# First attention: the early queries' values on four quarters of the PE array, with a second PSUM bank

## The chip, the cores and the metric

The kernel runs on one core of one Trainium2 chip. The metric is the device time of one execution in microseconds (us), shown as the median of several runs. The core has five engines with a program of their own each: PE (TensorE, matmuls and transposes; its weight loads are listed apart as PEld), DVE (VectorE), ACT (ScalarE), POOL (GpSimd) and SP (SyncE, here only a DMA queue). Matmuls write to PSUM, which has eight banks of 128 partitions x 512 fp32.

## The reference

A block of two layers on x of 32 sequences x 128 tokens x 128 features. Each layer adds an attention and then a feed-forward part to x, each conditioned on a vector per sequence. The change touches only the attention of the first layer:

```python
qkv = inputs @ W_qkv                       # 128 -> 3 x 16 heads x 64
q, k, v = jnp.split(qkv, 3, axis=-1)       # each reshaped to (b, l, H=16, D=64)
score = jnp.einsum('bihd,bjhd->bijh', q, k) / D ** 0.5
masked_score = score * mask + 1e+30 * (mask - 1.0)      # causal
wmat = jax.nn.softmax(masked_score, axis=2)
out = jnp.einsum('bijh,bjhd->bihd', wmat, v).reshape(b, l, H * D)
return out @ W_out
```

`inputs` is x modulated by the condition. The second layer's attention, its mixture of experts and its slot memory fill the second half of the run and are not touched.

## The kernel before

**Units.** The first attention works in 64 units: 16 values of h (a group g = h // 2 of four sequences, and one half of the 16 heads) times the four sequences b of the group. A unit has one sequence and eight heads. Since the mask is causal, the 64 early queries see only the 64 early keys, the 64 late queries see all 128 keys; the two are computed apart. A unit's eight heads are counted by slot (0 or 1), side (0 or 1) and par (0 or 1): head = 2 * (2 * slot + side) + par.

**Stages of a unit** (function `unit`), each delayed against the one before by a `Staggered` pipe with lags of 0, 3, 4 and 5 units, so that one step of the pipe issues `scores` of unit n, `turned` of unit n - 3, `values` of unit n - 4, and every fourth step `projected`:

- `scores`: 16 matmuls with 64 rows and 64 columns of the array into two banks, one for each par (the row half). The four (row half, column half) combinations follow one another in the order that `k % 2, (k // 2 + k) % 2` gives. Two matmuls add the mask. DVE takes the row maxima (`s_max`), and for the early queries subtracts the maximum into `s_sb` columns 4:6; ACT takes exp, four activations for the late queries and one for the early ones; POOL and DVE form the sums and scale.
- `turned`: six PE transposes of `s_sb` into two banks, four (late) read by one ACT copy, two (early) read by one DVE copy, into `pT`.
- `values`: one bank. Eight matmuls for the late queries (128 rows, 64 columns), then eight for the early ones (64 rows, 64 columns). An early matmul of par 0 uses row half 0 and column half 0, one of par 1 uses row half 1 and column half 1. One DVE copy of 128x512 takes the bank to `oT`.
- `projected`: 4 matmuls with `w_out` over four units' `oT`, added to x by DVE.

A matmul in fp32 stands in the trace as two instructions (a transpose as one), so the early values of a unit are 16 of them.

**V and its shifted copy.** `vv` (L460) keeps V of a sequence as `v` [keys, 8 heads, 64], and an SP DMA copies the early keys of the last four of its heads to partitions 64 to 127 of `vo`, so that row half 1 can work on early keys too. In this kernel the columns of W_qkv are permuted on the host, so that the last four heads in `v` are those of par 1.

**Banks.** Each `ps()` takes the next turn in a ring of eight, whose letters are three tile tags with 2, 3 and 3 banks; a turn waits until a bank of its tag has been read out:

```python
RING = "AABBBCCC"
def ps():
    if short:
        return bank("C")
    turn["all"] += 1
    return bank(RING[(turn["all"] - 1) % 8])
```

`short` is set after the last unit's scores, when the second layer's work begins to use A and B: the last four steps' `turned`, `values` and `projected` then have the three C banks only.

**What else lies in the stage.** Each step of the pipe is followed by three pieces of the next half's projections (`qk`: a 128x512 matmul and an ACT copy, or `v`), each of one turn. A step without anything else takes two turns for `scores`, two for `turned`, one for `values` and three for the pieces: eight. Into some steps the recurrence of the first feed-forward part is put (`recurrence`, seven times in this stage: three turns, sigmoids on ACT, and long DVE reciprocals and scans) or a cycle of its coupling network (`twisted`, seven cycles in this stage: a chain PE, ACT, PE, ACT with Gelu and Tanh, then DVE and POOL). They bring ACT table loads too. Engines' orders are those that the tile framework's scheduler makes out of the program's order and the waits; nearly all bank turns on PE start in the program's order (7 of 615 start ahead of an earlier one).

Of the kernel before, what the change touches and what calls it, by code (L numbers as in the profile page):

```python
# [16 lines left out]
ALU = mybir.AluOpType  # L17
AX = mybir.AxisListType

P = 128  # L20
B = 32
S = 128
D = 128
# [82 lines left out]
def _packs(i):  # L106

    g = lambda n: np.asarray(i[n])
    f = lambda n: g("L1_ffn_" + n)
    cond = g("cond_1024")  # L110
    c = lambda n: g("L1_cond_" + n)
# [39 lines left out]
        ("f_ln_g", _col(f("ln_g"))),  # L151
        ("f_ln_b", _col(f("ln_b"))),
    ]

    qkv = g("L0_attn_W_qkv")
    qkv_v = qkv[:, 2048:].reshape(D, 2, 4, 2, 64).transpose(0, 1, 3, 2, 4).reshape(D, 1024)
    attn0 = [
        ("w_qkv", np.concatenate([qkv[:, :2048], qkv_v], axis=1)),
    ]
    attn0o = [  # L160
        ("w_out", g("L0_attn_W_out").reshape(8, P, D).transpose(1, 0, 2).reshape(P, 8 * D)),
# [83 lines left out]
def program(ctx, tc, out, xT, packs, where):  # L245
# [19 lines left out]
    V, T, G, A = Pinned(nc.vector, pinned), Pinned(nc.tensor, pinned), Pinned(nc.gpsimd, pinned_g), nc.scalar  # L265
# [17 lines left out]
    def w(name):  # L283
        pack, rows, c0, n = where[name]
        return loaded[pack][:rows, c0 : c0 + n]
# [8 lines left out]
    def bank(tag):  # L294
        return psum.tile([P, 512], F32, tag="ps" + tag, name="ps", bufs=RING.count(tag))
# [6 lines that stand above are left out]
# [5 lines left out]
    def mm(out_, lhsT, rhs, start=True, stop=True):  # L307
        T.matmul(out_, lhsT=lhsT, rhs=rhs, start=start, stop=stop)

    def inner(ap, n):  # L310

        return ap.unsqueeze(2).to_broadcast([ap.shape[0], ap.shape[1], n])

    def outer(ap, n):

        return ap.unsqueeze(1).to_broadcast([ap.shape[0], n, ap.shape[1]])

    def tt(eng, out_, a, b, op):
        eng.tensor_tensor(out_, a, b, op)
# [10 lines left out]
    def col(g):  # L330
        return X[:, bass.ts(g, CH)]

    def b3(ap):

        return ap.rearrange("p (b s) -> p b s", s=S)

    def halves(ap):

        return ap.rearrange("p (u t) -> p u t", u=2)
# [34 lines left out]
    def act(*args, **kwargs):  # L374

        return tc.keep_in_program_order(A.activation(*args, **kwargs))  # L376
# [19 lines left out]
    w_qkv, w_out = w("w_qkv"), w("w_out")  # L396
    hTs, qks, vs, oTs = {}, {}, {}, {}
# [75 lines left out]
    def unit(h, b):  # L473

        g = h // 2
        cs = bass.ts(b, S)
        q2 = slice(b * S, b * S + 64), slice(b * S + 64, b * S + S)  # L480
        at = {}
        if b == 0:
            oTs[h] = apool.tile([P, 4, CH], F32, tag="oT", name="oT")

        def scores():

            two = [ps()[:, 0 : 3 * S].rearrange("p (c k) -> p c k", k=192) for par in range(2)]
            for late in (1, 0):
                for slot in range(2):
                    for k in range(4):  # L490
                        par, side = k % 2, (k // 2 + k) % 2
                        r = slice(64 * par, 64 * par + 64)
                        i = 2 * slot + side
                        o = two[par][64 * side : 64 * side + 64, slot, slice(0, S) if late else slice(S, 192)]
                        mm(o, qks[h][2 * i][r, q2[late]], qks[h][2 * i + 1][r, cs if late else q2[0]], start=bool(late) and slot == 0, stop=False)

            for par in range(2):
                mm(two[par][:, :, 64:192], twice16[:, 0, :], outer(causal16.rearrange("p u k -> p (u k)"), 2), start=False)

            s = apool.tile([P, 6, S], F32, tag="s_sb", name="s_sb", bufs=5)  # L500
            m6 = apool.tile([P, 2, 2, 3], F32, tag="s_max6", name="s_max6", bufs=5)
            nm = apool.tile([P, 2, 2], F32, tag="s_max", name="s_max", bufs=5)
            for par in range(2):
                V.tensor_reduce(m6[:, par], two[par].rearrange("p c (n k) -> p c n k", k=64), AX.X, ALU.max, negate=True)
                tt(V, nm[:, par], m6[:, par, :, 0], m6[:, par, :, 1], ALU.min)
                tt(V, s[:, 4:6, bass.ts(par, 64)], two[par][:, :, S:192], inner(m6[:, par, :, 2], 64), ALU.add)
                for slot in range(2):
                    act(s[:, 2 * par + slot], two[par][:, slot, 0:S], AF.Exp, bias=nm[:, par, slot : slot + 1])
            act(s[:, 4:6], s[:, 4:6], AF.Exp)
            sm = apool.tile([P, 8], F32, tag="s_sum", name="s_sum", bufs=5)  # L510
            late, early = s[:, 0:4], s[:, 4:6].rearrange("p c (n k) -> p (c n) k", k=64)
            if h == 2 * NCH - 1 and b >= CB - 2:

                V.tensor_reduce(sm[:, 0:4], late, AX.X, ALU.add)
                V.tensor_reduce(sm[:, 4:8], early, AX.X, ALU.add)
                V.reciprocal(sm, sm)
                tt(V, late, late, inner(sm[:, 0:4], S), ALU.mult)
                tt(G, early, early, inner(sm[:, 4:8], 64), ALU.mult)
            else:
                half = apool.tile([P, 4, 64], F32, tag="s_half", name="s_half")  # L520
                tt(G, half, late[:, :, 0:64], late[:, :, 64:128], ALU.add)
                part = apool.tile([P, 8, 32], F32, tag="s_part", name="s_part")
                tt(G, part[:, 0:4], half[:, :, 0:32], half[:, :, 32:64], ALU.add)
                tt(G, part[:, 4:8], early[:, :, 0:32], early[:, :, 32:64], ALU.add)
                V.tensor_reduce(sm, part, AX.X, ALU.add)
                V.reciprocal(sm, sm)
                tt(G, late, late, inner(sm[:, 0:4], S), ALU.mult)
                tt(G, early, early, inner(sm[:, 4:8], 64), ALU.mult)
            at["s"] = s

        def turned():
            pT = apool.tile([P, 6, S], F32, tag="pT", name="pT", bufs=3)
            p = ps()
            for i in range(4):
                T.transpose(p[:, bass.ts(i, S)], at["s"][:, i, :], ident)
            act(pT[:, 0:4], b3(p), AF.Copy)
            p = ps()
            for i in range(2):
                T.transpose(p[:, bass.ts(i, S)], at["s"][:, 4 + i, :], ident)
            V.tensor_copy(pT[:, 4:6], b3(p)[:, 0:2])  # L540
            at["pT"] = pT

        def values():
            p = ps()
            (v, vo), pT = vs[h][b], at["pT"]
            for late in (1, 0):
                for i in range(4):
                    slot, side = i // 2, i % 2
                    for par in range(2):
                        o = p[64 * par : 64 * par + 64, i * S + 64 * late : i * S + 64 * late + 64]  # L550
                        r = slice(0, P) if late else slice(64 * par, 64 * par + 64)
                        vh = v[r, 4 * par + i, :] if late or not par else vo[r, i, :]
                        mm(o, vh, pT[r, 2 * par + slot if late else 4 + slot, bass.ts(side, 64)])
            V.tensor_copy(oTs[h][:, :, cs], b3(p))

        def projected():
            u = h % 2
            p = ps()
            for m in range(4):
                mm(p, w_out[:, bass.ts(4 * u + m, D)], oTs[h][:, m, :], start=(m == 0), stop=(m == 3))  # L560
            tt(V, col(g), col(g), p, ALU.add)

        return [scores, turned, values] + ([projected] if b == CB - 1 else [])


# [278 lines left out]
    for h in range(NH):  # L844
# [3 lines left out]
        for b in range(CB):  # L848
# [15 lines left out]
            k = h - 6  # L864
# [581 lines left out]
    for r in range(NP):  # L1446
        a, c = 2 * r, 2 * r + 1
# [97 lines left out]
    for i in range(END + 2 * TURN):  # L1545
        r, k = i // TURN, i % TURN
# [62 lines left out]
```

## Time and profile before

| | us |
|---|---|
| median of 3 runs (1238.57 to 1244.77) | 1240.27 |
| profiled execution, its own time | 1240.42 |
| its span, first to last instruction | 1238.6 |
| first attention in it (first scores to last values) | 28 to 602 |
| PE busy | 1091.0 (88%) |
| DVE busy | 754.8 (61%) |
| ACT busy | 695.9 (56%) |
| POOL busy | 447.2 (36%) |

Busy PE is not PE at its peak: matmuls overlap, and their ends are modelled. A wait is read from the timeline, where a row is "start, length, engine, line, operation, out<-in, shape, count" and in brackets how long the engine had been idle and what released it. All helpers' instructions carry the helper's line (L259 for PE, DVE and POOL; L376 for most of ACT), so that they are told apart by the tiles' names: `ps` is any PSUM bank, `s_sb<-ps,s_max` on ACT the exp of late scores, `s_sb<-s_sb` that of early ones, `pT<-ps` the two copies of `turned`, `oT<-ps` that of `values`.

### The profile page before, as it was taken

What the parts mean: (1) busy time and instruction counts of PE and PEld (TensorE: products, weight loads), DVE (VectorE), ACT (ScalarE), POOL (GpSimd) and SP (SyncE); (2) the same over time, 40 slices, a digit from 0 to 9 for tenths busy, and PEclk for the clock granted to TensorE, in tenths of its full rate; (3) what the DMA queues carried; (4) which work ended last, traced back from release to release, by engine and by line L of the source; (5) the groups of instructions that cost most, each with busy time, mean ns of one, the idle gap of its engine ahead of it and who ended that gap; (6) DMA issues with size and microseconds to landing.
All of it is one profiled execution on the core that took longest, in us unless ns stands there. A gap on an engine that the chain in (4) does not pass through costs nothing. (4 is left out here: it accounts for less than half of the span.)

```text
span 1238.6 us, 28745 instructions
## 1 busy us (share of the span) xinstructions
PE 1091.0 (88%) x11429; PEld 696.8 (56%) x11429; DVE 754.8 (61%) x2253; ACT 695.9 (56%) x1668; POOL 447.2 (36%) x556
## 2 busy tenths in 40 slices
PE   6999999979999799888878668998999899998774
PEld 2556554535554355545545345776676676676543
DVE  2556766474884837837355388465756674657554
ACT  2655455555645555526355466666865587568631
POOL 1644545454554545524354531133213321222000
PEclk9999999989999899979989898999999999999867
DMA  7000000000000000000342300233023402320000
GB/s 278 11 10 10 12 8 10 10 4 10 8 10 10 4 7 10 11 3 8 110 121 66 100 26 3 78 112 129 11 78 103 154 12 69 104 67 11 2 17 17
DMA packets 23604, 56.46 MB, mean 46 GB/s; under 512 B 2608, under 2 KB 12976, under 8 KB 23344
## 3 DMA queue, kind: packets, MB, share of 16 engines
q0 software_dynamic: 9504, 38.97, 10.2%
q1 hardware_dynamic: 13248, 14.11, 3.8%
q8 instruction: 90, 1.47, 0.5%
q10 hardware_dynamic: 720, 1.57, 0.4%
q14 instruction: 42, 0.34, 0.1%
HBM read 46.25 MB, written 2.10 MB: 39 GB/s over the span
## 5 line engine op out<-in xcount | busy, mean ns | idle before, releaser
L376 ACT ACTIVATE s_sb<-ps,s_max 128x128 f32<-128x128 f32 x256 | 74.3, 368 | 123.0 <-DVE s_sb L259 116.8
L259 PE MATMUL ps<-hT,w_attn 128*128 128x512 f32 x256 | 128.7, 630 | 8.3 <-ACT s_sb L376 4.7
L259 POOL TENSOR_TENSOR s_sb<-s_sb,s_sum 128x512 f32<-128x512 f32 (+1 forms) x126 | 106.9, 869 | 67.9 <-DVE s_sum L259 54.7
L376 ACT ACT_TABLE_LOAD x63 | 80.8, 1283 | 79.9 <-DVE s_sb L259 53.5
L259 POOL DMA_INDIRECT ew<-in_expert,rows x64 | 63.5, 992 | 130.5 <-DVE ye L259 79.4
L376 ACT ACTIVATE qk<-ps 128x512 f32<-128x512 f32 x128 | 71.9, 610 | 48.6 <-PE ps L259 48.1
L259 POOL TENSOR_TENSOR s_half<-s_sb 128x256 f32<-128x256 f32 x62 | 46.8, 755 | 126.8 <-ACT s_sb L376 112.7
L259 PEld LDWEIGHTS ps<-qk 64*64 64x64 f32 x2048 | 54.6, 136 | 62.7 <-ACT s_sb L376 23.3
L376 ACT ACTIVATE he<-ps,ew 128x128 f32<-128x128 f32 x256 | 71.9, 386 | 31.8 <-issue 18.4
L259 PE MATMUL ps<-pT,v 128*64 128x64 f32 (+1 forms) x1536 | 85.1, 231 | 4.8 <-DVE X L259 3.1
L259 DVE TENSOR_REDUCE s_max<-ps 128x6 f32<-128x384 f32 x128 | 64.4, 540 | 39.0 <-PE ps L259 39.0
L259 PEld LDWEIGHTS ps<-pT,v 128*64 128x64 f32 (+1 forms) x1536 | 71.8, 140 | 23.4 <-issue 4.8
L259 PEld LDWEIGHTS ps<-hT,w_attn 128*128 128x128 f32 x256 | 47.4, 196 | 66.5 <-issue 42.8
L376 ACT ACTIVATE s<-ps,s1max 128x128 f32<-128x128 f32 x256 | 73.3, 391 | 18.9 <-DVE s1max L259 18.8
L259 PE MATMUL ps<-he,ew 128*128 128x128 f32 x512 | 77.1, 291 | 6.0 <-ACT he L376 5.1
L259 PEld LDWEIGHTS ps<-he,ew 128*128 128x128 f32 x512 | 67.9, 197 | 25.2 <-ACT he L376 13.7
L259 PE MATMUL ps<-qk 64*64 64x64 f32 (+1 forms) x2048 | 65.3, 255 | 16.1 <-ACT s_sb L376 13.8
L259 DVE TENSOR_REDUCE s_sum<-s_part 128x8 f32<-128x256 f32 x62 | 25.8, 417 | 84.7 <-POOL s_part L259 84.7
L259 PE MATMUL ps<-X,ew 128*128 128x128 f32 x512 | 76.8, 282 | 0.2 <-DMA ew<-in_expert,rows 0.2
L259 DVE TENSOR_REDUCE s1m<-ps 128x6 f32<-128x384 f32 x128 | 65.0, 548 | 16.2 <-PE ps L259 16.2
L259 PEld LDWEIGHTS ps<-X,ew 128*128 128x128 f32 x512 | 67.0, 193 | 10.4 <-issue 9.0
L259 PE MATMUL ps<-w_base,s 128*128 128x128 f32 x384 | 62.0, 288 | 7.9 <-ACT s L376 4.8
(302 smaller groups left out, 2544.3 us busy)
## 6 DMA issues: line engine op xcount, KB each, us to landing
vo<-v SPq DMA_DIRECT2D x64, 64.0 KB, 1.9
v1o<-v SPq DMA_DIRECT2D x8, 256.0 KB, 3.6
out_x<-ot SPq DMA_DIRECT2D x8, 256.0 KB, 2.3
X<-in_xT ACTq DMA_DIRECT2D x4, 256.0 KB, 9.1
X<-in_xT SPq DMA_DIRECT2D x4, 256.0 KB, 9.1
w_lowr<-in_lowr SPq DMA_DIRECT2D x1, 1024.0 KB
ew<-in_expert,rows POOLq DMA_INDIRECT x64, 5.1
w_ffn<-in_ffn SPq DMA_DIRECT2D x1, 928.0 KB, 8.4
```

The costliest lines, as they stand in the source:

```text
L259: ins = f(*args, **kwargs)
L376: return tc.keep_in_program_order(A.activation(*args, **kwargs))
```

## The change

Early matmuls of `values` use row half = slot and column half = par, all four quarters, in the same order of combinations as `scores`. Those of slot 1 write to a second bank `p2`; those of slot 0 stay in `p` with the late ones. So `values` takes two turns of the ring, and three DVE copies (128x256, and twice 128x128) take the place of one 128x512. The early part of `s_sb` is laid out by par instead of by slot (a DVE output of the same size), and the host no longer permutes the columns of W_qkv: the last four heads of `v`, which the DMA to `vo` copies, are now those of slot 1. The number of matmuls, transposes and DMAs and their sizes stay.

```diff
-    qkv = g("L0_attn_W_qkv")
-    qkv_v = qkv[:, 2048:].reshape(D, 2, 4, 2, 64).transpose(0, 1, 3, 2, 4).reshape(D, 1024)
     attn0 = [
-        ("w_qkv", np.concatenate([qkv[:, :2048], qkv_v], axis=1)),
+        ("w_qkv", g("L0_attn_W_qkv")),
     ]
...
-                tt(V, s[:, 4:6, bass.ts(par, 64)], two[par][:, :, S:192], inner(m6[:, par, :, 2], 64), ALU.add)
+                tt(V, halves(s[:, 4 + par]), two[par][:, :, S:192], inner(m6[:, par, :, 2], 64), ALU.add)
...
         def values():
-            p = ps()
+
+            p, p2 = ps(), ps()
             (v, vo), pT = vs[h][b], at["pT"]
-            for late in (1, 0):
-                for i in range(4):
-                    slot, side = i // 2, i % 2
-                    for par in range(2):
-                        o = p[64 * par : 64 * par + 64, i * S + 64 * late : i * S + 64 * late + 64]
-                        r = slice(0, P) if late else slice(64 * par, 64 * par + 64)
-                        vh = v[r, 4 * par + i, :] if late or not par else vo[r, i, :]
-                        mm(o, vh, pT[r, 2 * par + slot if late else 4 + slot, bass.ts(side, 64)])
-            V.tensor_copy(oTs[h][:, :, cs], b3(p))
+            for i in range(4):
+                for par in range(2):
+                    c = slice(64 * par, 64 * par + 64)
+                    mm(p[c, i * S + 64 : (i + 1) * S], v[:, 2 * i + par, :], pT[:, 2 * par + i // 2, bass.ts(i % 2, 64)])
+            for side in range(2):
+                for k in range(4):
+                    slot, par = k % 2, (k // 2 + k) % 2
+                    i, r, c = 2 * slot + side, slice(64 * slot, 64 * slot + 64), slice(64 * par, 64 * par + 64)
+                    o = p2[c, bass.ts(side, 64)] if slot else p[c, i * S : i * S + 64]
+                    vh = vo[r, 2 * side + par, :] if slot else v[r, 2 * i + par, :]
+                    mm(o, vh, pT[r, 4 + par, bass.ts(side, 64)])
+            o4 = oTs[h][:, :, cs]
+            V.tensor_copy(o4[:, 0:2], b3(p)[:, 0:2])
+            V.tensor_copy(o4[:, 2:4, 64:S], b3(p)[:, 2:4, 64:S])
+            V.tensor_copy(o4[:, 2:4, 0:64], halves(p2[:, 0:S]))
```

## The prediction

> **What bounds the kernel now.** I first read the busy times by stretch, because only the stage of the first attention (28 to 602 us of the span) is touched; the chain that ended last names its pieces only from 804.80 us on, so it says nothing about this stage. Columns are the stretch, its length, then each engine's busy time and count, and the granted clock:
>
> ```profile
> 100.00:150.00 50.00, 47.91 (x526) 28.42 (x526) 37.28 (x86) 26.03 (x63) 26.17 (x36) 1.00 0.03 8
> 150.00:200.00 50.00, 47.97 (x497) 28.00 (x496) 34.71 (x80) 26.54 (x63) 25.43 (x34) 1.00 0.05 12
> 250.00:300.00 50.00, 41.95 (x382) 23.06 (x382) 33.63 (x70) 24.41 (x52) 25.76 (x31) 0.86 0.03 7
> ```
>
> PE is busy 48 of 50 us in most stretches and 42 in some; DVE, the next, 33 to 37. So PE bounds the stage, except where something makes it wait. What does is in the waits of PEld from 50 to 620 us (total, times, longest); the timeline shows two such places, in a recurrence and in a cycle of the coupling network:
>
> ```profile
> PEld ps L259 <- ACT s_sb L376: 34.8, 38, 4.9
> ```
>
> ```profile
> 128.05 1.18 ACT L376 ACTIVATE s_sb<-ps,s_max 128x128 f32<-128x128 f32 x4 [3.08 <-DVE s_sb L259]
> ...
> 128.73 1.05 PE L259 MATMUL ps<-qk 64*64 64x128 f32 x32 [0.62 <-ACT s_sb L376]
> ...
> 129.11 0.42 ACT L376 ACTIVATE s_sb<-s_sb 128x256 f32<-128x256 f32 x1
> ...
> 129.42 0.60 ACT L376 ACTIVATE pT<-ps 128x512 f32<-128x512 f32 x1
> ```
>
> ```profile
> 277.16 1.56 PE L259 MATMUL ps<-qk 64*64 64x128 f32 x32 [4.09 <-ACT s_sb L376]
> ```
>
> The scores read no exp: they wait because the bank they want still holds scores whose exp ACT has not read. The ring explains it. Counting the program's turns, 29 of the 63 steps from one scores to the next have exactly eight, so there scores take the banks of the scores just before.
>
> **What the change does, part by part.** *Early matmuls.* This is the row rhythm of a unit's values before:
>
> ```profile
> 107.41 0.90 PE L259 MATMUL ps<-qk 64*64 64x128 f32 x32
> ...
> 108.24 0.39 PE L259 MATMUL ps<-causal,twice 128*128 128x256 bf16 x2
> ...
> 109.84 0.27 PE L259 MATMUL ps<-pT,vo 64*64 64x64 f32 x1
> ...
> 109.94 0.22 PE L259 MATMUL ps<-pT,vo 64*64 64x64 f32 x1
> ...
> 110.00 0.22 PE L259 MATMUL ps<-pT,vo 64*64 64x64 f32 x1
> ...
> 110.06 0.22 PE L259 MATMUL ps<-pT,vo 64*64 64x64 f32 x1
> ...
> 110.44 0.70 PE L259 MATMUL ps<-X,w_mix 128*128 128x512 f32 x1
> ```
>
> The two diagonal quarters start as a pair every 58 ns, eight pairs. The scores block already uses four quarters in the changed order: read record by record, its 16 early instructions of the same shape start in fours, the fours also 58 ns apart. Eight pairs become four fours: 4 x 58 = 0.23 us less per unit, 64 x 0.23 = **14.9 us** of PE at most. The gap on entering and leaving the 64-row form stays.
>
> *Copies.* Groups from 50 to 620 us (busy, mean ns):
>
> ```profile
> L259 DVE COPY oT<-ps 128x512 f32<-128x512 f32 x64 | 43.7, 682 | 6.7 <-remote 2.8 <-PE ps L259 2.0
> L259 DVE COPY pT<-ps 128x256 f32<-128x256 f32 x63 | 25.8, 410 | 0.0
> L259 DVE TENSOR_TENSOR s_sb<-ps,s_max 128x128 f32<-128x128 f32 x120 | 33.3, 281 | 0.0
> ```
>
> A line through the two copies gives 274 ns for 128x128, and the third row, another operation of that size, 281. So three copies are 410 + 274 + 274 = 958 ns for 682. A DVE instruction starts some 0.08 us before the end of the one ahead (the 0.41 us pT copy at 121.44 us, oT at 121.77), so from end to end it is 958 - 160 = 0.80 us, 0.12 more; ends of the range 0.12 and 0.28. Times 64: 7.7 us of DVE, hidden in most steps, since DVE has 13 to 17 us free in 50. Behind these copies stand the sums and the next maxima, for which ACT and then PE wait. The cover is gone in the seven recurrences, where reciprocals and scans keep DVE busy without a pause over about three units: 7 x 3 x 0.12 = **2.5 us**.
>
> Here a rule of the Trainium skill speaks against the change. "TensorEngine Tiling (Array Packing)", sections PSUM Bottleneck and Gotcha 1, says that tiling speeds TensorE but not the emptying of PSUM, that one access should span several tiles of a bank, and that different row tiles write to different banks. Were emptying the limit everywhere, the sum would be no gain and all 7.7 us lost: 1248.1. The rows do not show that on average, DVE being at 33 to 37 of 50, so I take 2.5. The rule's other half, the bank, is what I take over.
>
> *The second bank.* A plain step now takes nine turns of a ring of eight, and everything slides by one: s0 wants the former s1's bank, s1 that of the last transposes (free after ACT's pT copy), and the last projection piece wants the bank of the s0 of its own step. Steps of more turns slide likewise. On PE, in order, all later work queues behind such a wait: mask, transposes, values, pieces, then ACT's copies. Where ACT is on time this costs nothing: bank hand-overs have a median slack near 3 us before. Where ACT is late:
>
> - Recurrence: at 128.73 us scores start when s0's exps are done; the pT copy ends at 130.02. Wanting that bank, scores start 1.29 later, less the 0.15 that the block already loses inside (1.05 for 0.90): 1.1. In the next step a piece was stopped for 1.14 us at 138.47; one turn more puts one piece more (0.86) behind the same wait. They don't add, as ACT and DVE, which release, did not move: 1.0 per stretch.
> - Coupling cycle: at 277.16 scores wait for s0's exps and crawl (1.56) to 278.65; the pT copy that follows on ACT ends at 278.42. Starting there and taking 0.83, they end at 279.25: 0.6.
>
> Seven of each lie in the stage: 7 x 1.0 + 7 x 0.6 = **11.2 us**. The bounds are nothing (each tag has two or three banks, and whichever is free is taken) and some 24 us (about 24 turns, counted against the trace's release times, would be late by 0.8 to 2 us, if all added at 1.0).
>
> In these 14 stretches PE's saving of about two units each goes into the wait: 28 x 0.23 = 6.5, which leaves 14.9 - 6.5 = **8.4 us** of gain.
>
> *The end.* In the last four steps three C banks serve two transposes and one bank of values; with four, p2 needs the transposes' bank of its own step, hence an ACT copy, 0.6 us: 4 x 0.6 = **2.4 us**, between 0 and 6.
>
> *The rest:* the s_sb layout (281 ns, same size), the host's columns and the DMA to vo (64 KB, same) cost nothing: same instructions, no new wait.
>
> **Sum:** -8.4 + 11.2 + 2.5 + 2.4 = +7.7 us on the profiled execution's 1240.4: **1248**. It stands 0.15 us above the median of the runs, so the forecast for the median is the same.
>
> **Rivals.** *PE's gain comes through.* The order isn't rigid (at 181.98 us transposes went ahead of blocked scores), banks within a tag are interchangeable, and PE is the bound for 48 of 50 us. Then the waits don't lengthen: -14.9 + 2.5 to -8.4 + 2.5, or 1228 to 1234.5. Against it: 29 steps hand scores to scores now, and just these slide. *They cancel:* half of the bank and end cost, 6.8 - 8.4 + 2.5 = +1, 1241. *All late turns add:* every late turn delays PE by itself, +24 + 2.5 + 2.4 - 8.4 = +20, 1261; against it, the releases come from ACT and don't move with PE. *The quarters don't run together* (slot 0 and 1 in different banks, but each shared with other work): no gain, 1248 + 8.4 = 1256; against it, the scores' fours, which also write two banks.
>
> **Chances.** Forecast 0.35, gain comes through 0.25, cancel 0.22, all add 0.13, quarters fail 0.05. About 0.5% (6.2 us) is what a measurement can tell from no change. Faster: 0.25; same: 0.22; slower: 0.35 + 0.13 + 0.05 = 0.53. As signs are mixed: the forecast's own range is 1244 to 1254; the range for 8 in 10, 1231 to 1262, cuts off the better half of the gain and the far end of the adding case.
>
> **What would show it.** Early value records in fours 58 ns apart confirm the saving, pairs refute it. oT copies become 192, about 61 us busy for 43.7. PE's waits for ACT s_sb and pT (34.8 and 6.9 us in PEld's list) should grow by about 10 us, with pieces of qk and v waiting for s_sb. If they stay while the stage ends 8 or more us before 602, the bank step is wrong and the first rival right. If the stage is longer without such waits, the scheduler's order or DVE is the cause.

## The result and the profile after

Before, the median was 1239.83 us (14 runs, 1236.51 to 1244.88), after it 1244.28 us (14 runs, 1240.46 to 1247.66): a ratio of **1.0034, interval 1.0019 to 1.005**. A second series, with 22 runs of the change, gave 1.0031 (1.0019 to 1.0042). So the change costs some 4 to 5 us: a small loss, but one whose interval leaves out 1. The first profiled execution of the change took 1242.46 us (span 1240.7).

The page after, busy time by engine and the granted clock over the span:

```profile
PE 1085.4 (87%) x11429; PEld 686.7 (55%) x11429; DVE 756.7 (61%) x2381; ACT 694.4 (56%) x1668; POOL 446.9 (36%) x556
...
PEclk8999999989999889999889889999999999999867
```

The stretches that the prediction read (length, then busy time and count of PE, PEld, DVE, ACT, POOL, then the clock):

```profile
100.00:150.00 50.00, 47.48 (x528) 27.47 (x528) 36.13 (x98) 26.50 (x64) 25.89 (x36) 1.00 0.03 8
150.00:200.00 50.00, 47.74 (x496) 27.22 (x494) 34.44 (x93) 27.16 (x64) 25.37 (x36) 0.97 0.05 12
250.00:300.00 50.00, 41.51 (x346) 21.32 (x345) 32.64 (x80) 25.91 (x54) 26.82 (x33) 0.90 0.03 6
```

PE is a little less busy, DVE hardly changed, and the second stretch, at full clock before, has lost some. PEld's waits from 50 to 620 us (total, times, longest):

```profile
PEld ps L256 <- ACT s_sb L373: 38.8, 65, 3.2
PEld ps L256 <- DVE pT L256: 25.1, 10, 4.8
```

The wait for exp grew by 4 us and became shorter and more frequent; the wait for DVE's copy into pT, 4.5 us before, is new in this size. The values of a unit, and the copies behind them:

```profile
109.59 0.27 PE L256 MATMUL ps<-pT,vo 64*64 64x64 f32 x1
...
109.60 0.27 PE L256 MATMUL ps<-pT,v 64*64 64x64 f32 x1
...
109.69 0.22 PE L256 MATMUL ps<-pT,v 64*64 64x64 f32 x1
...
109.70 0.22 PE L256 MATMUL ps<-pT,vo 64*64 64x64 f32 x1
...
109.75 0.22 PE L256 MATMUL ps<-pT,v 64*64 64x64 f32 x1
...
109.81 0.22 PE L256 MATMUL ps<-pT,v 64*64 64x64 f32 x1
...
110.12 0.81 DVE L256 COPY oT<-ps 128x256 f32<-128x256 f32 x3
```

There are four starts, at 109.59, 109.69, 109.75 and 109.81. Each has two matmuls from `v` and two from `vo` (two row halves and two banks) within 20 ns; some of these rows are left out here. So they are fours, 58 ns apart once they run. Three copies take 0.81 us end to end. Groups from 50 to 620 us (busy, mean ns):

```profile
L256 DVE COPY oT<-ps 128x128 f32<-128x128 f32 x128 | 30.5, 277 | 0.1
L256 DVE COPY oT<-ps 128x256 f32<-128x256 f32 x64 | 26.3, 411 | 5.2 <-PE ps L256 5.2
```

**Where the time went.** Four kernels were profiled more than once. The table has, in us, the stage (start of the first scores to the start of the last projection's last matmul), what lies between that and the end of PE's last matmul, and POOL's wait ahead of `rb`, an operation of the second layer near 832 us:

| | stage | behind it | POOL before rb |
|---|---|---|---|
| before, 2 profiles | 579.1, 577.7 | 626.9, 627.0 | 4.57, 4.56 |
| idle turn and copies (form 7 below), 2 | 580.2, 575.9 | 629.0, 629.4 | 4.63, 4.64 |
| the change, 3 | 574.0, 579.2, 573.8 | 632.7, 632.0, 636.2 | 6.64, 6.35, 6.60 |
| by slot (change with two copies, form 6), 2 | 580.0, 579.4 | 626.0, 627.3 | 4.72, 4.60 |

On the mean the change's own stage is 2.7 us shorter (575.7 for 578.4), and all behind it, where no line was changed, 6.7 us longer (633.7 for 627.0). The sum, +4.0, is near the measured loss of some 4.5. The 2.7 is soft, since the stages overlap: one profile of the change has 579.2. What moves them is the time at half clock in the stage, 47.8 and 41.0 us before, 47.8, 61.4 and 47.8 in the change. With half of that taken off, an estimate from these figures, before has 555.2 and 557.2 us, the change 550.1, 548.5 and 549.9: at full clock the stage is 5 to 9 us shorter, 6.7 on the mean, and half clock takes part of it back.

### The profile page after: what moved, and what is told of

The parts are those of the page before. It is cut to its first block, busy times and chain, and to the rows that moved or that the text cites. A ratio compares the mean times of both kernels' runs of the same rounds, so it can differ in the third digit from the quotient of the medians.

```text
span 1240.7 us, 28947 instructions
## 1 busy us (share of the span) xinstructions
PE 1085.4 (87%) x11429; PEld 686.7 (55%) x11429; DVE 756.7 (61%) x2381; ACT 694.4 (56%) x1668; POOL 446.9 (36%) x556
## 5 line engine op out<-in xcount | busy, mean ns | idle before, releaser
L256 PEld LDWEIGHTS ps<-qk 64*64 64x64 f32 x2048 | 58.2, 136 | 79.4 <-DVE pT L256 24.6
L256 PE MATMUL ps<-qk 64*64 64x64 f32 (+1 forms) x2048 | 69.3, 254 | 19.4 <-DVE pT L256 18.2
L373 ACT ACTIVATE s<-ps,s1max 128x128 f32<-128x128 f32 x256 | 73.3, 391 | 20.1 <-DVE s1max L256 20.0
L256 PE MATMUL ps<-pT,v 128*64 128x64 f32 (+1 forms) x1536 | 71.7, 236 | 3.9 <-DVE X L256 3.8
L256 PE MATMUL ps<-w_attn,hT 128*128 128x512 f32 x128 | 69.4, 656 | 4.3 <-DVE tw L256 2.0
L256 PEld LDWEIGHTS ps<-pT,v 128*64 128x64 f32 (+1 forms) x1536 | 58.3, 142 | 22.2 <-issue 5.6
```

The costliest lines, as they stand in the source:

```text
L256: ins = f(*args, **kwargs)
```

## The experiments

Theories: the **bank theory** is the prediction's (the ring that slides by a turn costs 11 us), the **copies** are the second suspect, the **clock theory** says that PE's saved time comes back as idle time after which the granted clock halves. Forms 1 to 4 stood beside 24 runs of the kernel before (1239.46 us), 5 to 8 beside 51 (1239.77 us); ratios are to these.

**1. The idle turn**: the kernel before, with a turn that nobody uses.

```diff
         def values():
             p = ps()
+            turn["all"] += 1
```

> The kernel before, with one idle turn of the ring after each bank of values: the ring slides as in the change, nothing else changes. Bank theory: the waits for banks cost here what they cost in the change, with no PE saving against them: 7 to 14 us slower than before, with the waits of PE for ACT's exps and pT copy up by about as much. Rival (the slide is harmless, what was lost comes from the copies or behind the stage): within 2 us of before.

Measured: 1238.51 us, **0.9994 (0.9977 to 1.0011)**. The ring slides here as in the change, and nothing is lost: the size that the bank theory gave the slide is refuted.

**2. The copies alone**: one bank, 128x512 copied as 128x256, 128x128 and 128x128.

```diff
-            V.tensor_copy(oTs[h][:, :, cs], b3(p))
+            o4 = oTs[h][:, :, cs]
+            V.tensor_copy(o4[:, 0:2], b3(p)[:, 0:2])
+            V.tensor_copy(o4[:, 2:4, 64:S], b3(p)[:, 2:4, 64:S])
+            V.tensor_copy(o4[:, 2:4, 0:64], b3(p)[:, 2:4, 0:64])
```

> The kernel before, with its one bank of values read by three DVE copies (256, 128 and 128 columns) and nothing else changed. Bank theory: the copies cost 2.5 us. DVE rival: emptying PSUM is what costs, 5 to 8 us (64 x 0.12 and more). If they are all hidden: 0.

Measured: 1239.23 us, **0.9991 (0.9974 to 1.0007)**. Alone they cost nothing that can be measured.

**3 and 4. The second bank from tag C, outside of the ring**; in 4 the late values are split by slot too, so that two copies of 128x256 do.

```diff
-            p, p2 = ps(), ps()
+            p, p2 = ps(), bank("C")
```

> The changed kernel, but its second bank is taken from the three C banks without a turn of the ring, so that nothing slides. Bank theory: the ring's waits go and the PE saving stays: 7 to 11 us below the changed kernel, so 3 to 7 us below before. Rival (slide harmless): as the changed kernel, within 2 us. Rival behind the stage (what the first attention gains is lost again later, since what feeds the experts does not come earlier): the stage ends 5 us or more before that of the kernel before, and the total is the same within 2 us.

> As the kernel with the second bank outside the ring's turns, but late values are split by slot too: slot 0 wholly in the first bank, slot 1 wholly in the second, so that two DVE copies of 128x256 empty them in place of three. By durations 410 + 410 less 80 ns of overlap are 0.74 us a unit for 0.80: 0.06 x 64 = 4 us of DVE less, of which some 1 us counts. Bank theory: 0 to 2 us below the kernel with three copies. DVE rival: 3 to 5 us below it.

Measured: 1264.1 us, 1.0194 (1.0176 to 1.0212), and 1266.16 us, 1.0218 (1.02 to 1.0235). Both miss: meant to take the slide away, they lose 25 us. Compared with before, scores of 3 fall behind mostly over recurrences (2.5 and 4.2 us in the two steps of two units at the first one, 5.8 at the second), where DVE's order is another too. What of it is the crowded tag and what the order isn't separated. They say nothing for the bank theory, since with the idle turn the slide itself is free.

**5. The saved work put back**: the early matmuls of the change issued twice.

```diff
-            for side in range(2):
+            for side in (0, 1, 0, 1):
```

> The changed kernel with every early value matmul issued a second time, to the same place: PE gets back the 0.23 us a unit that the quarters saved, with bank turns and copies as in the change. Clock theory (the saved time turns into longer waits of PE, and a stretch with more idle PE is followed by half clock): 3 to 6 us below the changed kernel, near 1239 to 1241, with a mean granted clock near 0.946 instead of 0.939, although PE has more to do. Bank or copy theory: not faster than the changed kernel, and up to 9 us slower where PE is the bound.

Measured: 1264.07 us, 1.0184 (1.016 to 1.0209). Inconclusive: with the doubled cost the scheduler made another order. At the first recurrence DVE's maxima stand behind more of the long scans, at 129.68 us for 122.84 in the change and 126.45 in before. How much of the 24 us is this order and how much the added work isn't separated. A run that adds work changes the plan as well as the work.

**6. By slot, in the ring**: the change with its turn, but slot 0 of the late values wholly in `p`, slot 1 in `p2`, and two copies of 128x256.

```diff
-                    mm(p[c, i * S + 64 : (i + 1) * S], v[:, 2 * i + par, :], pT[:, 2 * par + i // 2, bass.ts(i % 2, 64)])
+                    mm((p, p2)[i // 2][c, i % 2 * S + 64 : (i % 2 + 1) * S], v[:, 2 * i + par, :], pT[:, 2 * par + i // 2, bass.ts(i % 2, 64)])
...
-                    o = p2[c, bass.ts(side, 64)] if slot else p[c, i * S : i * S + 64]
+                    o = (p, p2)[slot][c, side * S : side * S + 64]
...
-            V.tensor_copy(o4[:, 2:4, 64:S], b3(p)[:, 2:4, 64:S])
-            V.tensor_copy(o4[:, 2:4, 0:64], halves(p2[:, 0:S]))
+            V.tensor_copy(o4[:, 2:4], b3(p2)[:, 0:2])
```

> The changed kernel, second bank with its turn of the ring as there, but late values split by slot too, so that two DVE copies of 128x256 take the place of three copies: 0.74 for 0.80 us a unit. Copy theory: the copies matter, 2 to 4 us below the changed kernel. Clock theory: PE's savings are the same and its waits nearly so, within 2 us of it.

Measured: 1239.99 us, **1.0001 (0.9989 to 1.0012)**: as before, and 4.8 us under the change run beside it. That is more than the copy theory allowed, and the clock theory, which expected the change's time within 2 us, misses.

**7. The idle turn and the three copies**, without the quarters: the edits of 1 and 2 in one kernel, all of the change but its gain.

> The kernel before with the idle turn and the three copies together: all of the change but the quarters and the second bank itself. Clock theory: within 2 us of before (both parts were within 1 us alone), clock as before. Copy or ring theory (the two only hurt together): 4 to 6 us above before, as the change.

Measured: 1242.22 us, 1.0007 (0.9994 to 1.0021). By medians it is 2.4 us above before, though its interval takes in 1. So bank turns and copies together don't make the whole loss (the change is 2.6 us above this form), but a part of it may be theirs.

**8. The change again**, unaltered, beside forms 5 to 7.

> The changed kernel once more, on the same chip as these. All theories: ratio 1.002 to 1.005 to before. Clock theory: mean granted clock 0.935 to 0.942, below that of before in the same call (0.947), and the runs' times fall in order of their clocks; the first attention ends, counted from its first scores, 3 to 5 us earlier than in before.

Measured: 1244.79 us, **1.0031 (1.0019 to 1.0042)**; median clock 0.938, where the runs of before beside it have 0.949, form 6 0.942 and form 7 0.947. The forecast of a stage 3 to 5 us shorter misses: it took 579.2 us, as long as before's.

The engines' orders of 7 and of the change are nearly the same (value matmuls aside, some ten of PE's 9381 instructions stand elsewhere), so their difference is mainly that of the quarters. At the second recurrence (two of the texts below call it the third), PE in 7:

```profile
181.68 0.89 PE L259 MATMUL ps<-qk 64*64 64x128 f32 x16 [1.14 <-DVE pT L259]
```

In 8, and in the first profile of the change, with what follows there (start, us, wait in brackets):

```profile
177.58 0.88 PE L256 MATMUL ps<-qk 64*64 64x128 f32 x16 [1.58 <-DVE pT L256]
```

```profile
180.71 0.89 PE L256 MATMUL ps<-qk 64*64 64x128 f32 x16 [1.59 <-DVE pT L256]
...
181.84 1.91 PE L256 MATMUL ps<-w_attn,hT 128*128 128x512 f32 x2
...
183.68 1.53 PE L256 MATMUL ps<-qk 64*64 64x128 f32 x16
```

The wait has grown from 1.14 to 1.58 us, by 0.44: what two units save. DVE's pT comes when it comes; PE is only there earlier. And in the first profile the work behind the wait runs at half speed (1.91 us for two matmuls of 128x512 that take 1.02 elsewhere). In that profile all changes of the clock lie on a grid of 3.41 us. Cut along it (PE busy first; the clock follows POOL's busy time):

```profile
174.83:178.24 3.41, 3.41 (x67) 2.55 (x59) 3.41 (x5) 0.43 (x1) 0.75 (x1) 1.00 0.02 5
178.24:181.65 3.41, 1.82 (x21) 0.92 (x20) 3.41 (x9) 2.56 (x6) 1.84 (x3) 1.00 0.00 0
181.65:185.07 3.42, 3.42 (x20) 1.88 (x19) 2.63 (x8) 2.75 (x7) 2.34 (x4) 0.50 0.01 2
```

PE was busy for 1.82 of 3.41 us, and the clock was halved for the next step of the grid. In 8 the grid lies otherwise, and the same wait falls into two of its steps:

```profile
173.59:177.00 3.41, 2.41 (x24) 1.00 (x20) 3.41 (x7) 1.04 (x1) 2.52 (x2) 1.00 0.02 5
177.00:180.42 3.42, 2.84 (x37) 1.95 (x38) 3.26 (x10) 3.41 (x10) 1.95 (x3) 1.00 0.00 0
```

Neither is followed by half clock. So a wait of that length makes half clock possible, and where the grid lies has a part in it. The cost is small here: the two units with the wait take 1.6 us longer than in 8 (15.37 for 13.74), but the next two 0.8 less.

**9 to 12. Second and third profiles**, one execution each: the change, by slot, before, and the idle turn with the copies, all unaltered. They ask whether the wait ahead of `rb` comes again.

> A further profile of the kernel with the change. Clock theory: the wait for pT in the third recurrence is 1.6 us again, as in both profiles of it, but whether the clock halves behind it is left to chance (it did in one of two); the stage's length goes with its half-clock time, some 0.5 us per us of it. Rival, a lasting loss behind the stage: POOL's wait ahead of rb near 833 us is 6.4 to 6.6 us again, not the 4.6 of before, and costs PE some 2 us there in every execution.

> A second profile of the form with the values split by slot and two copies. Clock theory: the same 1.6 us wait for pT, and half-clock time within 10 us of the 149 of its first profile. Rival: POOL's wait ahead of rb is 4.7 us again, about 2 us under that of the change.

> A second profile of the kernel before. Clock theory: the waits of PE stand where they stood, within 0.1 us, and only half-clock stretches move, so that the stage takes 575 to 583 us (579.1 in the first profile). Rival: POOL's wait ahead of rb is 4.6 us again; if it is 6.5 here, that wait is chance and no part of the change.

> A second profile of the form with the idle turn and the three copies, without the quarters. Clock theory: the wait for pT in the third recurrence is 1.14 us again, 0.44 under the change's, with no half clock behind it, and the stage is 576 to 584 us. Rival: POOL's wait ahead of rb is 4.6 us again.

Measured: the four took 1245.67, 1243.18, 1239.12 and 1239.78 us in that one execution, which is too few to rank them. The wait for pT was 1.58 us in 9, with half clock behind it, 1.59 in 10, without, and 1.15 in 12; the stages are in the table (12's is 0.1 us short of what was expected). The rival holds: `rb` waited 6.60, 4.60, 4.56 and 4.64 us. POOL's rows and PE's that wait for them, in 9, and behind them in 11:

```profile
834.40 1.04 POOL L256 TENSOR_TENSOR rb<-xabT,w_base 64x512 f32<-64x512 f32 x1 [6.60 <-DMA ew<-in_expert,rows]
...
835.50 1.12 PE L256 MATMUL ps<-rb,xabT 32*128 32x512 f32 x2 [1.73 <-POOL rb L256]
...
836.55 1.90 PE L256 MATMUL ps<-he,ew 128*128 128x128 f32 x8
...
838.38 2.07 PE L256 MATMUL ps<-rb,xabT 32*128 32x512 f32 x2
```

```profile
831.67 1.04 POOL L259 TENSOR_TENSOR rb<-xabT,w_base 64x512 f32<-64x512 f32 x1 [4.56 <-ACT he L376]
...
833.00 1.12 PE L259 MATMUL ps<-rb,xabT 32*128 32x512 f32 x2
```

In the change `rb` waits for a fetch of experts' weights (`ew`), and PE waits for `rb`. In before too: the row names ACT, but in all of 9 to 12 `rb` starts 0.16 us behind the landing of `ew` (in 11 at 826.04 + 5.47 us). So what differs is how late the fetch lands. In two of the three profiles of the change PE's work then runs at half clock, here again behind a wait. Between two fixed marks of PE around this place before took 12.6 us in both profiles, the idle turn with the copies 12.6 twice, by slot 12.6 twice, but the change 15.9, 14.2 and 17.6; 14.2 is the profile without half clock. That is 3.3 us of the 6.7.

Why is the fetch late? Transfers in 1.3 us around the issue of `v1o`, a write of values that follows the fetch by 1.3 us, in the first profile of the change and at the same distance in 11 (queue: packets, MB, share; then the issue with us to landing):

```profile
q8 instruction: 1, 0.02, 4.7%
issues: line engine op xcount, KB each, median us to landing
v1o<-v SPq DMA_DIRECT2D x1, 256.0 KB, 6.8
```

```profile
q0 software_dynamic: 11, 0.05, 31.4%
issues: line engine op xcount, KB each, median us to landing
v1o<-v SPq DMA_DIRECT2D x1, 256.0 KB, 5.2
ew<-in_expert,rows POOLq DMA_INDIRECT x1, 5.5
```

In the change a 16 KB packet of the instruction queue, a piece of the program's code, starts while the fetch and the 256 KB write `v1o` are under way, and these land 1.3 to 2 us later (9 has 7.5 us for the fetch). In all three profiles of the change the packet starts within 0.43 us of the issue of `v1o`; in the eight of before, the idle turn, the copies, 6 and 7 it starts 3.7 to 5.7 us after it, and there `rb` waits 4.5 to 4.7 us, except for 5.4 with the copies alone, whose packet came first of the eight (3.7) and whose `v1o` took 6.7 us as well. In 3, 4 and 5 the packet starts 4.2 us after, 7.9 before and 2.4 before, and `rb` waits 4.5, 4.5 and 5.0. By slot has a packet of 8 KB within 0.4 us of `v1o`, without delay. So the loss at `rb` looks like a coincidence of transfers and not like work that the values add. That the code packet is the cause fits these fourteen profiles but isn't shown: no run moved it by itself. Why it comes where it does in the change, and which engine's code it is, stays open.

## Why the prediction was right or wrong

Its number was 1248, on the right side and 4 us off. Its reasons hold less well: the stage that it put 7.7 us later came 2.7 earlier on the mean, and the loss is in a place that it never looked at. That the number was near is luck.

- **Early matmuls: right.** The fours are there. From one start of scores to that two units later, steps that nothing disturbs (six of them up to 176 us) are 0.44 us shorter in all profiles of the change, 0.22 per unit for the 0.23 of the sum; with the idle turn, the copies or both, these steps are unchanged to 0.01.
- **What is absorbed: right in kind, too small.** Compared with form 7 (third profile against second), of 31 steps 11 keep the full 0.44 and four about half of it: 11 x 0.44 + 0.9 = 5.7 us; the other steps move both ways, by up to 2.7 us. The prediction kept 8.4. PE's idle time in 28 to 602 us says the same: 48 us in before, 43 in 7 and 52 in the change, so 9 us of the saving went into waits for the 6.5 of the sum.
- **The second bank: wrong, the step that failed.** "7 x 1.0 + 7 x 0.6 = 11.2" took each late turn as lost. The late turns are there, but behind another engine, and they replace other waits. At the first recurrence, in before and in the change:

```profile
121.90 1.23 PE L259 MATMUL ps<-qk 64*64 64x128 f32 x32 [0.23 <-DVE pT L259]
```

```profile
121.65 0.88 PE L256 MATMUL ps<-qk 64*64 64x128 f32 x16 [1.52 <-DVE pT L256]
...
128.29 0.61 ACT L373 ACTIVATE pT<-ps 128x512 f32<-128x512 f32 x1
...
129.00 0.76 PEld L256 LDWEIGHTS ps<-qk 64*64 64x64 f32 x32 [0.76 <-ACT pT L373]
```

  The scores at 129.00 are those for which 1.1 us was forecast. Their weight loads do wait for ACT's pT copy, but PE is at work until then. PE waited at the scores of the unit before, at 121.65, for 1.52 us and for DVE's copy into pT (0.23 in the kernel before). The step to these scores is 0.74 us longer than before, in the idle turn as in the change, but the next is 0.81 and 0.79 shorter: PE catches up. Over 28 to 602 us, PE's own waits in us, by what ended them (one figure for each profile):

| ended by | before | idle turn | the change |
|---|---|---|---|
| DVE's copy into pT | 7.1, 8.3 | 17.5 | 20.2, 20.1, 20.1 |
| ACT's exps | 19.2, 19.1 | 12.0 | 15.9, 16.1, 15.9 |
| ACT's Gelus of the coupling network | 10.8, 10.8 | 5.8 | 6.2, 6.1, 6.2 |
| all waits over 0.15 us | 46.1, 46.9 | 41.2 | 51.3, 51.4, 51.2 |

  The slide alone adds some 10 us of waits, about what the sum had, and takes away 12 us of others. The sum charged the first and never asked for the second. It multiplied a delay by seven without asking what ends the stretch.
- **Copies: duration right, cost wrong.** 0.81 us end to end for the 0.80 of the sum, but 2.5 us of lost time for a measured 0.9991 (0.9974 to 1.0007). The rows on DVE's free time were the better guide than the rule on emptying PSUM that was set against them.
- **The end: about right.** From the last pair's scores to the last projection before has 35.2 and 33.9 us, the change 36.6 in all three: 2.1 us for the 2.4 of the sum. Against form 7 (32.9 and 31.5) it is 4.4, so the size depends on the comparison.
- **Left out: the rest of the program and the clock.** Behind the stage the sum had nothing. There stand +6.7 us, of which 3.3 are at `rb`. Of the other 3.4, form 7 has some 2.2 too, without the quarters and without a loss at `rb`; what makes them isn't shown. Half clock behind the stage took 75 and 78 us in before, 82, 84 and 92 in the change, but 78 and 91 in form 7 and 81 and 85 by slot, so it doesn't sort the forms. The change's runs tend to follow their clock, from 1240.5 us at 0.945 to 1247.6 at 0.934. That the saved time itself lowers the clock behind the stage isn't shown: by slot has the quarters and as much half clock in its stage (55 us twice, for 48, 61 and 48), and keeps before's time.
- **Rivals.** "PE's gain comes through" fell to what was absorbed and to the loss at `rb`; "they cancel" (1241) has the time of by slot, though by another sum than the one forecast; "all late turns add" and "the quarters don't run together" are refuted by the idle turn and by the fours.

Since two errors, +11 in the stage and -7 behind it, took each other away, the time is no proof of the theory. No form tried is faster than before beyond its interval. The quarters without a second bank were not tried: before's pairs write from two row halves into one bank, but to different partitions of it.

## What to carry to other kernels

Before a late turn is charged once per stretch, ask which engine ends that stretch: PE that comes late to a place where it would have waited loses nothing, and PE that comes early gains nothing. Count the waits that a shift takes away as well as those that it adds. Read more than one profile before a few us are put down to a line: here one place, two hundred us behind the change, held about half of what was lost behind the stage, in three profiles of three and in none of the six others that were measured there. And judge a rearranged stage by forms that carry one part of it each, in the same order of instructions, since a form that alters modelled costs gets another order, and the forms here that did so lost 24 to 27 us.

## What the runs showed of the hardware

The granted clock moves between 1.0 and 0.5 in stretches of 3.41 us and multiples, on a grid that is fixed within an execution and lies otherwise in the next, and it fell behind a wait of only 1.6 us, PE having been busy for 1.82 of 3.41 us. Counted over all fourteen profiles, a step of the grid at full clock with PE busy for less than 1.4 us, as the profile gives it, was followed by half clock in 228 cases of 228, one with 1.4 to 2.2 us in 85 of 281, and one with more in 13 of 3945. Full clock came back only behind steps with 2.5 us or more. Within the middle band busy time alone doesn't decide: in the second profile by slot a step with 1.83 us of PE, in few long matmuls, was followed by full clock. "TensorE: Matmul & The Clock Gate" of the Trainium skill, section "Part 1: The HAM clock gate", has the two levels and this free-running window, but gives at least one idle window as the condition for the drop; here partly busy steps were enough, and the measurement decides. Half clock took 126 to 151 us of the spans of about 1240 us of before, the change, by slot and the idle turn with the copies.

Packets of program code travel among the data: where one of 16 KB started during a gather's first 1.5 us, the gather took 7.5 us to landing, for 5.5 in the kernel before. That the one causes the other isn't shown.
